# Padding the parts of a graph aggregation so that all its matmul operands begin at multiples of 64 bytes

## Chip, cores, metric

One core of one Trainium2 chip. The metric is the device time of one execution in microseconds (us). The kernel before takes 974.26 us (median of the 3 runs that were known when the prediction was made, 972.87 to 974.94); over all 6 runs of that comparison 973.04 us.

## The reference, cut to what matters

Two layers of attention over a graph of 4096 nodes with 512 features. Layer 0 attends inside 32 blocks of 128 nodes. Layer 1 is a graph attention with 8 heads of 64, in which the softmax over the neighbours j of node i needs only exp(t_j), because the term of i cancels:

```python
    def _L1_gnn_ref(x, adj, W, a_origin, a_dst):
        mx = jnp.einsum('nf,hfd->hnd', x, W)
        s_i = jnp.einsum('hnd,hd->hn', mx, a_origin)
        t_j = jnp.einsum('hnd,hd->hn', mx, a_dst)
        logits = s_i[:, :, None] + t_j[:, None, :]
        masked = jnp.where(adj[None] > 0, logits, neg_inf)
        attn = jax.nn.softmax(masked, axis=-1)
        out_h = jnp.einsum('hij,hjd->hid', attn, mx)
```

So layer 1 is a product of the 0/1 adjacency mask (4096 x 4096) with a matrix of 522 columns per node: 512 weighted features, 8 weights for the denominators and 2 of padding.

## The kernel before

A "part" is one tile of 128 nodes of that matrix, as a sum of two terms (high and low) of the 4-byte matmul type fp32r, in 3 chunks of 2 x 174 columns. The preparation makes the parts tile by tile: norm of the row (VectorE), transpose and projection with the weights (TensorE), weighing with exp(t) (VectorE), split into the two terms (ScalarE and GpSimd). The aggregation multiplies the transposed mask of a row of nodes (`at`, stationary) with all 32 parts (moving), 96 matmuls per row and 32 rows.

```python
CB = 3
CW1 = 174
EW = CB * CW1
# ... cut ...
    def split(e, dst):
        e3 = e.rearrange("p (c w) -> p c w", c=CB)
        nc.scalar.copy(dst[:, :, 0, :], e3)
        nc.gpsimd.tensor_sub(dst[:, :, 1, :], e3, dst[:, :, 0, :].bitcast(F32))
# ... cut: in aggregate, four loads of mw ...
        nc.vector.transpose(at8 ..., mw ...)          # arguments cut
        at = sb.tile([P, NT, P], F32R, name="at")
        nc.vector.tensor_copy(at ..., at8 ...)        # arguments cut
        pg = ps_g.tile([P, CB, 512], F32, name="pg")
        for j in range(NT):
            for c in range(CB):
                nc.tensor.matmul(
                    pg[:, c, : 2 * CW1], at[:, j, :],
                    part(j)[:, c].rearrange("p s w -> p (s w)"),
                    start=(j == 0), stop=(j == NT - 1),
                )
# ... cut ...
    with ExitStack() as straight:
        pool1 = straight.enter_context(tc.tile_pool(name="l1", bufs=1))
        sb2 = straight.enter_context(tc.tile_pool(name="sb2", bufs=2))
        lo = straight.enter_context(tc.tile_pool(name="lo", bufs=LO // 2))
        # ... cut: layer 0, and the preparation of the parts ...
        sb3 = straight.enter_context(
            tc.tile_pool(name="sb3", bufs=2, side="right", reuse_waits="tile")
        )
        for i in range(NT):
            row = sb3.tile([P, D], F32, name="row3", bufs=1)
            nc.sync.dma_start(row, x1_d[i])
            tot = aggregate(sb3, ps_g, i, lambda j: parts[j])
            # ... cut ...
            if i == 1:
                graphs_are_tiles(sb3)
                hold(0, rs_all, 1.0 / S_MAX, ALU.is_ge)
                # ... cut: three more range checks
```

A scheduler decides the order of the instructions on each engine, and the pools decide which buffers share addresses. Both matter below. If a check fails, a slow exact branch runs after the straight one.

Of the kernel before, what the change touches and what calls it, by code (L numbers as in the profile page):

```python
# [9 lines left out]
F32 = mybir.dt.float32  # L10
F32R = mybir.dt.float32r
# [9 lines left out]
P = 128  # L21
# [15 lines left out]
CB = 3  # L37
CW1 = 174
EW = CB * CW1
NEG = -1.0e6  # L40
EPS = 1e-5
SCALE = float(D) ** -0.5
# [9 lines left out]
def kernel(  # L52
# [185 lines left out]
    def project1(ps_m, hT, w1x):  # L238

        pm = [ps_m.tile([P, D], F32, name="pp") for _ in range(2)]  # L240
        for g, n in ((1, HW + H), (0, HW)):
            for k in range(KC):
                nc.tensor.matmul(  # L243
                    pm[g][:, :n], hT[:, k, :], w1x[:, k, g * HW : g * HW + n],
                    start=(k == 0), stop=(k == KC - 1),
                )
        return pm
# [11 lines left out]
    def aggregate(sb, ps_g, i, part):  # L259
# [21 lines left out]
        for j in range(NT):  # L281
            for c in range(CB):
# [4 lines left out]
                )  # L287
        tot = sb.tile([P, EW], F32, name="tot")
        tot3 = tot.rearrange("p (c w) -> p c w", c=CB)
# [8 lines left out]
    def graphs_are_tiles(sb):  # L298


        ptr_i = sb.tile([1, NPTR], I32, name="ptr_i", bufs=1)
        nc.sync.dma_start(ptr_i, ptr)
        ptr_f = sb.tile([1, NPTR], F32, name="ptr_f", bufs=1)
        nc.vector.tensor_copy(ptr_f, ptr_i)
        ends_i = sb.tile([1, NT, 2], I32, name="ends_i", bufs=1)
        nc.gpsimd.iota(ends_i, pattern=[[P, NT], [P - 1, 2]], base=0, channel_multiplier=0)
        ends = sb.tile([1, NT, 2], F32, name="ends", bufs=1)
        nc.vector.tensor_copy(ends, ends_i)
        ge = sb.tile([1, NT, 2], F32, name="ge", bufs=1)
        for t0 in range(0, NT, 4):  # L310
            cmp = sb.tile([1, 8, NPTR], F32, name="cmp", bufs=1)
            nc.vector.tensor_tensor(
                cmp,
                ends[:, t0 : t0 + 4].rearrange("p t e -> p (t e)")[:, :, None].to_broadcast(
                    [1, 8, NPTR]
                ),
                ptr_f[:, None, :].to_broadcast([1, 8, NPTR]),
                ALU.is_ge,
            )
            nc.vector.tensor_reduce(  # L320
                ge[:, t0 : t0 + 4].rearrange("p t e -> p (t e)"), cmp, AX.X, ALU.add
            )
        same = sb.tile([1, NT], F32, name="same", bufs=1)
        nc.vector.tensor_tensor(same, ge[:, :, 0], ge[:, :, 1], ALU.is_equal)
        later = sb.tile([1, NT - 1], F32, name="later", bufs=1)
        nc.vector.tensor_tensor(later, ge[:, 1:, 0], ge[:, : NT - 1, 1], ALU.is_gt)
        good = sb.tile([1, 2], F32, name="good", bufs=1)
        nc.vector.tensor_reduce(good[:, 0:1], same, AX.X, ALU.min)
        nc.vector.tensor_reduce(good[:, 1:2], later, AX.X, ALU.min)
        nc.vector.tensor_tensor(held[0:1, 6:7], good[:, 0:1], good[:, 1:2], ALU.mult)  # L330
# [8 lines left out]
    w1x = None  # L339
    parts = []  # L340
    with ExitStack() as straight:
        pool1 = straight.enter_context(tc.tile_pool(name="l1", bufs=1))
        sb2 = straight.enter_context(tc.tile_pool(name="sb2", bufs=2))
        lo = straight.enter_context(tc.tile_pool(name="lo", bufs=LO // 2))

        with ExitStack() as prep:
            ps_t = prep.enter_context(tc.tile_pool(name="ps_t0", bufs=3, space=PSUM))
            ps_p = prep.enter_context(tc.tile_pool(name="ps_p0", bufs=4, space=PSUM))

            def part_tile(pool, j):  # L350
                if j >= LO:
                    return pool.tile([P, CB, 2, CW1], F32R, name=f"part{j}")
                if j % 2 == 0:
                    two.append(pool.tile([P, 2, CB, 2, CW1], F32R, name=f"part{j}", tag="lo"))
                return two[-1][:, j % 2]

            two = []

# [8 lines left out]
            def prepare(i, hT, part):  # L367
                pm = project1(ps_p, hT, w1x)
                e = sb2.tile([P, EW], F32, name="e")
                nc.gpsimd.memset(e[:, EC:], 1.0)  # L370
# [6 lines left out]
            with (  # L377
# [49 lines left out]
                def read(i, diag, sums):  # L427
# [4 lines left out]
                    for h in range(2):  # L432
# [7 lines left out]
                        for c0, c1 in pieces:  # L440
                            if c0 < c1:
                                junk = sb.tile([P, NH], BF16, name="junk", bufs=1)
                                nc.scalar.activation(  # L443
                                    junk[:, c0:c1], a[:, c0:c1], AF.Exp, scale=2.0 * NEG,
                                    accum_out=sums[:, n : n + 1],
# [15 lines left out]
                def scores(g, hT, gT, r, diag, sums, counts):  # L461

                    pss = ps_s.tile([P, G, P], F32, name="pss")
                    for t in range(G):
                        for k in range(KC):
                            nc.tensor.matmul(  # L466
                                pss[:, t, :], gT[:, k, ts(t, P)], hT[:, k, ts(t, P)],
                                start=(k == 0), stop=(k == KC - 1),
                            )
                    s = sb.tile([P, G, P], F32, name="s")  # L470
                    nc.vector.scalar_tensor_tensor(s, diag, 2.0, pss, ALU.mult, ALU.add)
                    for t in range(G):
                        nc.scalar.activation(
                            s[:, t, :], s[:, t, :], AF.Exp, bias=r[:, t : t + 1],
                            accum_out=sums[t][:, 0:1],
                        )
                        rsum = rs_all[:, G * g + t : G * g + t + 1]
                        nc.vector.tensor_reduce(rsum, sums[t][:, : counts[t]], AX.X, ALU.add)
                        nc.vector.reciprocal(rsum, rsum)
                    return s  # L480
# [44 lines left out]
                for g in range(NG):  # L525
# [12 lines left out]
                    def prepare_on(now):  # L538
                        if now:
                            i = len(ahead)  # L540
                            ahead.append(normed1(i))
                            if i:
                                prepare(i - 1, ahead[i - 1], part_tile(lo, i - 1))

                    s = scores(g, hT, gT, r, *look)
# [23 lines left out]
            for i in range(n - 1, NT):  # L569
                hT = nhT  # L570
                if i + 1 < NT:
                    nhT = normed1(i + 1)
                prepare(i, hT, part_tile(lo if i < LO else hi, i))
# [16 lines left out]
        for i in range(NT):  # L590
# [21 lines left out]
# [3 lines that stand above are left out]
                hold(1, rs_all, 1.0 / S_MIN, ALU.is_le)  # L615
                e_flat = e_all.rearrange("p t h -> p (t h)")
                hold(2, e_flat, E_MIN, ALU.is_ge)
                hold(3, e_flat, E_MAX, ALU.is_le)
# [13 lines left out]
    with tc.If(bad > 0):  # L632
# [67 lines left out]
        with (  # L700
# [10 lines left out]
            with tc.For_i(0, NT, 1) as i:  # L711
# [8 lines left out]
                for c in range(N // CW):  # L720
# [12 lines left out]
                    f = sb.tile([P, CW], F32, name="f")  # L733
                    nc.vector.tensor_scalar(f, sm, 1.0 - NEG, NEG, ALU.mult, ALU.add)
                    nc.vector.tensor_tensor(ac, qk, f, ALU.mult)
# [7 lines left out]
                for c in range(N // CW):  # L743
# [7 lines left out]
                    for u in range(CW // P):  # L751
                        j = c * (CW // P) + u
# [11 lines left out]
        with (  # L764
# [60 lines left out]
            with tc.For_i(0, n_levels, 1):  # L825
                with (
# [11 lines left out]
                    nc.vector.tensor_scalar(te, te, 0.0, None, ALU.min)  # L838
                    e = sb.tile([P, EW], F32, name="e")
                    nc.gpsimd.memset(e[:, EC:], 1.0)  # L840
# [68 lines left out]
```

## Time and profile before

| what | before |
|---|---|
| time, median of 6 runs | 973.04 us |
| TensorE (PE) busy | 940.3 us of 970.5 us |
| aggregation, first to last matmul start | 468.74 to 958.04 us |
| one row of 96 matmuls | 15.293 us, 159.30 ns a matmul |
| last projection ends, to first aggregation matmul | 467.56 to 468.74 us |

The lines of the page that carry this stand in the prediction. Start times are those of the matmul records in the trace; the step from one start to the next is used because the end of a matmul is modelled. "Half clock" means a record of a granted TensorE clock of 0.5. "Seam" is the passage from the preparation to the aggregation.

One stretch of the timeline of before is needed for what follows (start, duration, engine, line, operation; in brackets the idle time before it and what ended it). It shows how work for the aggregation's second row sits in the middle of the preparation:

```profile
373.12 2.26 DVE L277 CAST at<-at 128x4096 fp32r<-128x4096 fp8e4 x1
...
376.06 0.65 DVE L114 BATCH_NORM_STATS2 stats<-row 128x6 f32<-128x512 f32 x1
...
377.64 1.44 DVE L121 TENSOR_SCALAR row<-row,mv,rstd 128x512 f32<-128x512 f32 x1 [0.94 <-POOL rstd L120]
...
379.14 1.12 PE L127 MATMUL pt<-ident,row 128*128 128x128 f32 x4 [3.02 <-DVE row L121]
```

The cast of `at` occupies VectorE (DVE) for 2.26 us, the norms of the next rows come after it, and PE waits 3.02 us for a normalised row. A half-clock record of 3.4 us follows from 378.7 us on.

### The profile page before, as it was taken

The numbers are of one execution on the slowest core, as the hardware profiler recorded it, in microseconds if no ns is written. First come the engines' busy times: TensorE is split into PE (matmuls) and PEld (weight loads), VectorE is DVE, ScalarE is ACT, GpSimd is POOL, SyncE is SP. The second block draws the span as 40 slices with busy tenths as digits, with TensorE's granted clock in tenths as the row PEclk, the third lists the DMA queues.
The fourth block names the chain that finished last, engine by engine and source line by source line (L and its number), as shares of the span: only waits on it lengthen the run. The fifth ranks groups of instructions, "written<-read, shape, count | busy, mean of one in ns | idle before, by whom it ended". The sixth has DMA issues, their size and how long they took to land.

```text
span 970.5 us, 13180 instructions
## 1 busy us (share of the span) xinstructions
PE 940.3 (97%) x5051; PEld 817.5 (84%) x5051; DVE 459.4 (47%) x978; ACT 260.7 (27%) x505; POOL 184.0 (19%) x344
## 2 busy tenths in 40 slices
PE   8999999989999998999999999999999999999995
PEld 5676677766677776788999999999999999999994
DVE  4678777866766358655133242433424233242321
ACT  5865666665762222233100000000000000000000
POOL 2211113231122125555110110101011010110100
PEclk9999999999999999999999999999999999999998
DMA  9989889898883033221022312223131221312201
GB/s 343 419 346 378 322 329 364 355 369 317 336 339 148 33 104 108 72 66 55 1 76 56 88 50 82 62 69 87 44 87 52 80 85 47 87 49 82 61 27 37
DMA packets 58042, 148.28 MB, mean 153 GB/s; under 512 B 6386, under 2 KB 23026, under 8 KB 49778
## 3 DMA queue, kind: packets, MB, share of 16 engines
q1 hardware_dynamic: 48178, 130.31, 38.3%
q10 hardware_dynamic: 9792, 17.05, 4.6%
q8 instruction: 41, 0.67, 0.3%
q14 instruction: 31, 0.25, 0.1%
HBM read 113.77 MB, written 33.55 MB: 152 GB/s over the span
## 4 chain that ended last, share of the span: by engine, by line
PE 89%; DVE 3%; DMA 2%; POOL 2%; ACT 2%; issue 1%; SPq 0%; ACTq 0%; DVEq 0%; POOLq 0%
PE pg L283 50%; PE pp L420 11%; PE pp L408 10%; PE pp L243 9%; PE pp L493 3%; PE pss L466 3%; PE pt L127 2%; DMA row<-x_d 1%; POOL part L231 1%; DMA xg<-x 1%; DVE a L136 1%; ACT junk L443 1%; DVE row L121 0%; DVE stats L114 0%; POOL rstd L120 0%
## 5 line engine op out<-in xcount | busy, mean ns | idle before, releaser
L283 PE MATMUL pg<-part,at 128*128 128x348 f32 x3072 | 489.6, 321 | 1.2 <-DVE e L252 1.2
L283 PEld LDWEIGHTS pg<-part,at 128*128 128x128 f32 x3072 | 489.4, 188 | 1.5 <-issue 1.5
L277 DVE CAST at<-at 128x4096 fp32r<-128x4096 fp8e4 x32 | 74.0, 2313 | 312.2 <-PE pg L283 312.2
L290 ACT COPY tot<-pg 128x522 f32<-128x522 f32 x32 | 19.2, 599 | 470.5 <-PE pg L283 470.5
L443 ACT ACTIVATE junk<-a 128x2048 bf16<-128x2048 f32 (+15 forms) x92 | 124.4, 1352 | 48.7 <-DVE x L495 28.0
L243 PE MATMUL pp<-w1x,hT 128*128 128x256 f32 (+1 forms) x512 | 118.4, 385 | 0.0
L420 PE MATMUL pp<-wv,hT 128*128 128x512 f32 x256 | 116.6, 600 | 0.0
L408 PE MATMUL pp<-hT,m_sb 128*128 128x256 f32 x512 | 113.2, 379 | 0.0
L243 PEld LDWEIGHTS pp<-w1x,hT 128*128 128x128 f32 x512 | 95.7, 192 | 13.6
L408 PEld LDWEIGHTS pp<-hT,m_sb 128*128 128x128 f32 x512 | 96.1, 190 | 12.9 <-issue 0.5
L420 PEld LDWEIGHTS pp<-wv,hT 128*128 128x128 f32 x256 | 49.1, 192 | 61.9 <-issue 61.9
L136 DVE TENSOR_SCALAR a<-a 128x512 fp8e4<-128x512 f32 x256 | 98.2, 460 | 0.5 <-DMA a_d<-a 0.4
L595 POOL COPY den_all<-tot 128x1 f32<-128x1 f32 x31 | 5.8, 186 | 369.1 <-DVE tot L291 369.1
L128 ACT ACTIVATE hT<-pt 128x512 f32<-128x512 f32 x64 | 37.0, 598 | 68.8 <-PE pt L127 68.7
L604 POOL TENSOR_TENSOR tot<-tot,row 128x512 f32<-128x512 f32 x31 | 40.0, 1290 | 61.7 <-DVE tot L296 61.7
L231 POOL TENSOR_TENSOR part<-e,part 128x522 fp32r<-128x522 f32 x32 | 42.1, 1316 | 43.0 <-ACT part L230 38.8
L118 POOL TENSOR_SCALAR ve<-mv 128x1 f32<-128x1 f32 x64 | 18.7, 295 | 150.9 <-DVE mv L116 150.8
L252 DVE TENSOR_TENSOR e<-pp,e 128x256 f32<-128x256 f32 x64 | 26.6, 417 | 28.9 <-ACT e L371 25.2
L270 DVE STREAM_TRANSPOSE at<-mw 128x1024 f32<-128x1024 f32 x32 | 39.5, 1236 | 0.0
L120 POOL TENSOR_TENSOR rstd<-ve,neghalf 128x1 f32<-128x1 f32 x64 | 38.5, 604 | 4.4
L424 DVE TENSOR_TENSOR v<-pp,bv_sb 128x512 f32<-128x512 f32 x32 | 22.0, 688 | 36.0 <-PE pp L420 36.0
L412 ACT ACTIVATE gT<-pp,c_sb 128x256 f32<-128x256 f32 x64 | 29.7, 468 | 29.4 <-PE pp L408 29.3
(93 smaller groups left out, 584.1 us busy)
## 6 DMA issues: line engine op xcount, KB each, us to landing
a<-adj SPq DMA_DIRECT2D x64, 1024.0 KB, 13.1
a_d<-a SPq DMA_DIRECT2D x32, 512.0 KB, 10.6
row<-x_d SPq DMA_DIRECT2D x64, 256.0 KB, 3.5
mw<-a_d SPq DMA_DIRECT2D x128, 128.0 KB, 4.0
xg<-x SPq DMA_DIRECT2D x16, 512.0 KB, 4.7
x_d<-x ACTq DMA_DIRECT2D x32, 256.0 KB, 4.2
out<-tot ACTq DMA_DIRECT2D x31, 256.0 KB, 3.8
wkT_sb<-wkT SPq DMA_DIRECT2D x4, 256.0 KB, 6.3
```

Of the source, the lines that this page charges most:

```text
L120: nc.gpsimd.tensor_tensor(rstd, ve, neghalf, ALU.pow)
L128: nc.scalar.activation(dst, pt, AF.Relu)
L136: nc.vector.tensor_scalar(a8v[:, u], av[:, u], 0.0, None, ALU.is_gt, saturate=False)
L231: nc.gpsimd.tensor_sub(dst[:, :, 1, :], e3, dst[:, :, 0, :].bitcast(F32))
L243: nc.tensor.matmul(pm[g][:, :n], hT[:, k, :], w1x[:, k, g * HW : g * HW + n], start=(k == 0), stop=(k == KC - 1),)
L270: nc.vector.transpose(at8.rearrange("p c n b -> p (c n b)").bitcast(F32).rearrange("p (c u n) -> p c u n", c=NW, n=B), mw.rearrange("p u ( ...
L277: nc.vector.tensor_copy(at.rearrange("p (c b) q -> p c b q", b=BY), at8.rearrange("p c q b -> p c b q"))
L283: nc.tensor.matmul(pg[:, c, : 2 * CW1], at[:, j, :], part(j)[:, c].rearrange("p s w -> p (s w)"), start=(j == 0), stop=(j == NT - 1),)
L408: nc.tensor.matmul(pp[:, : G * P], m_sb[:, k, ts(m, P)], hT[:, k, :], start=(k == 0), stop=(k == KC - 1),)
L420: nc.tensor.matmul(pp, hT[:, k, ts(t, P)], wv[:, k, :], start=(k == 0), stop=(k == KC - 1))
L443: nc.scalar.activation(junk[:, c0:c1], a[:, c0:c1], AF.Exp, scale=2.0 * NEG, accum_out=sums[:, n : n + 1],)
L604: nc.gpsimd.tensor_add(num, num, row)
```

## The change

The intent: let every moving operand (a chunk of a part) and every stationary operand (`at`) begin at a multiple of 64 bytes. A chunk of 348 floats gets the room of 352, and a two-element tile grows to 64 bytes so that what is allocated after it, `at` included, is aligned. The padded parts need 1.5 KB more per partition, for which the left-hand pools of layer 1's weights and norm buffers move to the right-hand side and end with the preparation.

```diff
+CP = 352
...
-        good = sb.tile([1, 2], F32, name="good", bufs=1)
+        good = sb.tile([1, 16], F32, name="good", bufs=1)
...
     with ExitStack() as straight:
-        pool1 = straight.enter_context(tc.tile_pool(name="l1", bufs=1))
-        sb2 = straight.enter_context(tc.tile_pool(name="sb2", bufs=2))
         lo = straight.enter_context(tc.tile_pool(name="lo", bufs=LO // 2))
 
         with ExitStack() as prep:
+            pool1 = prep.enter_context(tc.tile_pool(name="l1", bufs=1, side="right"))
+            sb2 = prep.enter_context(tc.tile_pool(name="sb2", bufs=2, side="right"))
...
             def part_tile(pool, j):
                 if j >= LO:
-                    return pool.tile([P, CB, 2, CW1], F32R, name=f"part{j}")
-                if j % 2 == 0:
-                    two.append(pool.tile([P, 2, CB, 2, CW1], F32R, name=f"part{j}", tag="lo"))
-                return two[-1][:, j % 2]
+                    t = pool.tile([P, CB, CP], F32R, name=f"part{j}")
+                else:
+                    if j % 2 == 0:
+                        two.append(pool.tile([P, 2, CB, CP], F32R, name=f"part{j}", tag="lo"))
+                    t = two[-1][:, j % 2]
+                return t[:, :, : 2 * CW1].rearrange("p c (s w) -> p c s w", s=2)
```

## The prediction

> **What bounds the kernel now.** I read the page's busy shares first, then its slices, its chain and its costliest groups, then waits and windows of single stretches.
>
> ```profile
> PE 940.3 (97%) x5051; PEld 817.5 (84%) x5051; DVE 459.4 (47%) x978; ACT 260.7 (27%) x505; POOL 184.0 (19%) x344
> ...
> PE   8999999989999998999999999999999999999995
> ...
> PE 89%; DVE 3%; DMA 2%; POOL 2%; ACT 2%; issue 1%; SPq 0%; ACTq 0%; DVEq 0%; POOLq 0%
> PE pg L283 50%; PE pp L420 11%; PE pp L408 10%; PE pp L243 9%; PE pp L493 3%; PE pss L466 3%; PE pt L127 2%; DMA row<-x_d 1%; POOL part L231 1%; DMA xg<-x 1%; DVE a L136 1%; ACT junk L443 1%; DVE row L121 0%; DVE stats L114 0%; POOL rstd L120 0%
> ...
> L283 PE MATMUL pg<-part,at 128*128 128x348 f32 x3072 | 489.6, 321 | 1.2 <-DVE e L252 1.2
> L283 PEld LDWEIGHTS pg<-part,at 128*128 128x128 f32 x3072 | 489.4, 188 | 1.5 <-issue 1.5
> L277 DVE CAST at<-at 128x4096 fp32r<-128x4096 fp8e4 x32 | 74.0, 2313 | 312.2 <-PE pg L283 312.2
> ```
>
> TensorE (PE) is busy for 97% of the span and is 89% of the chain that ended last. Half of the chain is one line, the aggregation's product: 3072 matmuls of 348 fp32r columns, which run from 468.7 us to 958 us with one wait of 1.2 us in front of them. Nothing feeds them late: the cast that makes their stationary operand waits 312 us in total for PE, not the other way round. So 489.6 us are set by the rate of that stream alone, and every nanosecond per matmul is worth 3.07 us.
>
> The windows view of L283, with the columns length, PE busy (count), PEld busy (count), granted clock, DMA share and GB/s, shows that the rate is steady:
>
> ```profile
> 500.00:600.00 100.00, 100.00 (x630) 100.00 (x629) 1.00 0.25 68
> 700.00:800.00 100.00, 100.00 (x629) 100.00 (x628) 1.00 0.25 72
> ```
>
> Some 628 starts in 100 us is 159.3 ns a matmul (first to last start: 489.3 us / 3071), at full granted clock. The starts in the trace repeat from row to row within a nanosecond: every row of 96 matmuls takes 15.293 us. That is not traffic from elsewhere; the matmuls' own operands decide it.
>
> Ahead of it, layer 1's preparation (projection L243, norm, split) also runs near PE's speed. Waits of PE from 345 to 500 us:
>
> ```profile
> PE pt L127 <- DVE row L121: 5.6, 4, 3.0
> PE pg L283 <- DVE e L252: 1.2, 1, 1.2
> ```
>
> **What the Trainium skill says.** (1) "TensorE: Matmul & The Clock Gate", section "Wait — 56ns, not 53.3ns?": back to back, a warm matmul costs N ÷ 2.4 GHz + about 2.5 ns. For N = 348 that is 147.5 ns. The trace has 159.3 ns, so 11.8 ns (36 us over the stage) are unexplained. The fp32 products of layer 0 have no such excess: 512 columns start 429 ns apart and 256 columns 216 ns apart, which is 2 clock cycles a column plus 2.3 ns. Only the fp32r stream, which takes a 4-byte column every cycle, falls behind. (2) "SBUF — State Buffer", section "Specifications (TRN2)": cachelines are 16 bytes. All operands of the products begin at multiples of 16 already, so this page gives the change no reason to help. (3) The same page, section "Operand start alignment", asks only for element alignment, and says of its runs that they timed nothing: no page states a gain at 64 bytes.
>
> **The change part by part.**
> *Alignment.* From the built programs: before, the 96 moving operands of a row begin at 0, 16, 32 and 48 bytes past a multiple of 64 (30, 18, 30 and 18 of them; a chunk is 348 x 4 = 1392 bytes = 21.75 x 64), and the stationary operand always at 32. After, all begin at 0. The count and the width of the matmuls stay. I sorted the time from each start to the next by where the moving operand begins: 159.0 ns at 0, 160.2 at 16, 159.5 at 32, 158.7 at 48. The third that is aligned already is not faster. Letting neighbours' alignments in too (a fit over the 96 matmuls of a row, each averaged over 29 rows) makes a fully aligned one 1.3 to 2.3 ns cheaper. Taken at face value that is 3/4 of about 1.5 ns x 3072 = some 3.5 us gained. What the trace can't tell is the stationary operand, since it is at 32 in all 3072 matmuls, nor what happens when both are aligned together.
> *The allocation.* The right-hand pools now hold layer 1's weights, norm and split buffers, and the aggregation's buffers lie over them. In the built order of before, the first two adjacency rows' transposes and casts, and the check of the graph's bounds, stand well inside the preparation. In that of after, all of them follow the last part. On DVE, after the last weighing: four pairs of the range checks (about 0.18 + 0.18 twice, 0.29 + 0.42 twice = 2.1 us), a copy that waits for an iota on GpSimd, which stands behind the last split (1.24 us, from 469.4 in the trace of before) and takes 0.27 us, then the transpose (1.23 us) and the cast (2.3 us). Chained onto before's times: last projection ends 467.6, last split ends about 470.3, iota 470.6, copy 470.8, the rest of the checks to 472.9, transpose to 474.1, cast (behind a small cast) to 476.8. The first aggregation matmul starts at 476.9 instead of 468.7: **+8.2 us**. The other copies are no trouble: 15.3 us of matmuls per row hide them.
> *What the move gives back.* Before, that early work on DVE delayed the norms: the two larger waits in the preparation are 3.0 us at 376.1 and 1.5 us at 395.2, and the first is followed by a record of half clock for 3.4 us, which costs 1.7 us of PE. Without the casts in the way up to 6.2 us come back; I count 4.5 of them.
> *The clock.* "TensorE: Matmul & The Clock Gate", section "What's actually happening", has idle windows of about 3.4 us bring the clock to half. The trace of before agrees: its idle spells of 2.5 and 3.0 us each precede 3413 ns at half clock. A spell of 9 us before the aggregation should do so too: + 1.7 us.
> Sum without a change of rate: 8.2 + 1.7 - 4.5 = +5.4 us; with the small gain of the fit, about +2 us.
> *The padded parts themselves* cost nothing in time: split's copies and subtractions write the same 522 elements, into three pieces as before.
>
> **The rivals.**
> A, the rate hardly moves (the sum above): 974 to 982 us. For it speaks that the aligned third isn't faster.
> B, the read of operands is the limit and counts 64-byte lines. A moving operand covers 22 or 23 of them (22.5 on average), a weight load at 32 covers 9, at 0 it covers 8. If 31.5 lines take 159.3 ns, 30 take 151.7 ns: 7.6 x 3.07 = 23 us gained, less 5: about 956 us. For it: only the stream with the doubled rate of bytes is short of its ideal, and the small, repeating differences between starts (152 to 168 ns) depend on addresses. Against it: parts that begin at 0 cover 68 lines in their three chunks and those at 32 cover 67, but the former are faster (476.7 against 479.1 ns).
> C, both operands aligned brings the ideal of 147.5 ns: 36 us gained, less 5, about 943 us. For it: the change goes to the length of widening a two-element tile to keep the stationary operand aligned too, which looks like knowledge of a measured effect. Against it: the trace shows nothing of it.
> D, the same phase in every pair of weight load and stream makes them collide more: 3 ns more would be 983 to 988 us. The address-dependent differences allow it.
> E, the aggregation starts late by more than I count, since a row's load or cast lands in the second row too: at most some 5 us more.
>
> **Range and chances.** I give A 0.6, B and C together (with what lies between) 0.33, D and E 0.07. A centres on 978 us, B and C on 945 to 957, some of it short of 2%. A gain of 2% needs under 954.8 us, thus about 25 us from the rate (8 ns a matmul): I take 0.28 for that. Slower by 2% needs over 993.7 us: 0.04. The middle of this lopsided mix is about 971 us; eight in ten between 942 and 985.
>
> **What would show it.** In the profile after: the L283 group's busy time (489.6 now; 485 to 490 under A, about 466 under B, about 453 under C) and the count of starts in 100 us (628; 659; 678). The wait of PE's first pg matmul should grow from 1.2 us to about 9 us, ended by the cast of at, with a half-clock record after it; the waits for DVE row L121 from 345 us on should shrink from 5.6 us to under 2. If the first pg wait stays under 3 us my reading of the moved order is wrong; if the repeating pattern of starts turns into one constant gap, the address-dependent part was alignment. The prediction fails mainly if the unexplained 11.8 ns do come from the stationary operand's place, which this trace cannot exclude.

## The result, and the profile after

| | before | after |
|---|---|---|
| time, median of 6 runs each | 973.04 us | 971.95 us |
| ratio of the fast runs, 95% interval | | 0.9987 (0.9974 to 1.0) |
| last projection ends | 467.56 us | 461.15 us |
| first aggregation matmul starts | 468.74 us | 469.81 us |
| first row of 96 | 15.37 us | 17.45 us |
| every later row of 96 | 15.293 us | 15.200 us |
| last aggregation matmul starts | 958.04 us | 958.30 us |

A ratio is the mean time of one kernel's fast runs over that of the other's in the same rounds, so it is not quite the ratio of the medians quoted. The time is the same within the noise. In later rounds, with 14 runs of the changed kernel against 19 of before, the ratio was 0.9995 (e12 below).

The page after, in the lines that answer to those in the prediction (TensorE's line number has moved from L283 to L284, the cast's from L277 to L278):

```profile
PE 938.7 (97%) x5051; PEld 816.8 (84%) x5051; DVE 459.2 (47%) x978; ACT 260.6 (27%) x505; POOL 177.0 (18%) x344
...
PE 92%; DVE 2%; DMA 2%; ACT 1%; issue 1%; POOL 0%; SPq 0%; DVEq 0%
...
L284 PE MATMUL pg<-part,at 128*128 128x348 f32 x3072 | 488.8, 321 | 8.7 <-DVE at L278 8.7
L284 PEld LDWEIGHTS pg<-part,at 128*128 128x128 f32 x3072 | 488.6, 188 | 9.0 <-issue 9.0
L278 DVE CAST at<-at 128x4096 fp32r<-128x4096 fp8e4 x32 | 73.4, 2292 | 298.2 <-PE pg L284 298.2
```

The aggregation's busy time is hardly shorter (488.8 against 489.6 us), but the idle time in front of it has grown from 1.2 to 8.7 us, and the cast of its first stationary operand ends it. PE's waits from 345 to 500 us were two lines before; after, they are one:

```profile
PE pg L284 <- DVE at L278: 8.7, 1, 8.7
```

The windows view of L284 shows the rate: 633 or 634 matmuls that overlap 100 us, where before it was 629 or 630.

```profile
500.00:600.00 100.00, 100.00 (x634) 100.00 (x633) 1.00 0.23 65
600.00:700.00 100.00, 100.00 (x633) 100.00 (x633) 1.00 0.26 73
```

The timeline of after where the preparation ends:

```profile
454.64 6.51 PE L244 MATMUL pp<-w1x,hT 128*128 128x264 f32 x29
...
462.43 1.22 POOL L232 TENSOR_TENSOR part<-e,part 128x522 fp32r<-128x522 f32 x1 [2.14 <-ACT part L231]
463.60 0.27 POOL L307 IOTA ends_i<- 1x64 int32 x1
463.91 0.18 DVE L309 CAST ends<-ends_i 1x64 f32<-1x64 int32 x1 [2.21 <-POOL ends_i L307]
...
466.10 1.24 DVE L271 STREAM_TRANSPOSE at<-mw 128x1024 f32<-128x1024 f32 x1
...
467.37 2.29 DVE L278 CAST at<-at 128x4096 fp32r<-128x4096 fp8e4 x1
...
469.81 8.43 PE L284 MATMUL pg<-part,at 128*128 128x348 f32 x38 [8.66 <-DVE at L278]
```

DVE stands idle for 2.21 us for the iota, which GpSimd (POOL) issues behind the last split; then come the range checks, the transpose and the cast, all while PE has nothing to do. The clock's records show half clock from 464.3 to 474.6 us, so the first 4.8 us of matmuls run slowly and the first row takes 17.45 us. The windows from 450 to 480 us, before and then after, show it in the granted clock (the third figure from the end):

```profile
450.00:480.00 30.00, 28.83 (x158) 26.22 (x157) 8.30 (x20) 5.49 (x13) 9.97 (x19) 1.00 0.05 18
```

```profile
450.00:480.00 30.00, 21.34 (x105) 19.57 (x104) 18.80 (x39) 4.01 (x9) 6.42 (x12) 0.83 0.16 42
```

**Where the time went**, from the two profiled runs: from the start of the fifth part's projection to the end of the last one, the preparation takes 140.8 instead of 148.9 us, -8.1 (its waits for the norms and their half clock are gone); the first matmul then waits 8.66 instead of 1.17 us, +7.5; the first row is 2.1 us longer; each of the other rows is 0.093 us shorter, -2.9 over 31 of them. The sum is -1.4 us, near the -1.1 us of the medians. In these two runs the last matmul starts 0.26 us later all the same, because the profiled run of after is already 1.7 us late when that fifth projection starts (320.4 against 318.7 us). This is not put down to the change: in the other profiled runs with the pools on the right that point lies anywhere from 316.0 to 320.6 us. Four effects of 2 to 8 us cancel.

### The profile page after: what moved, and what is told of

It is laid out like the page before. It is cut to its first block, busy times and chain, and to the rows that moved or that the text cites. A ratio compares the mean times of both kernels' runs of the same rounds, so it can differ in the third digit from the quotient of the medians.

```text
span 970.4 us, 13183 instructions
## 1 busy us (share of the span) xinstructions
PE 938.7 (97%) x5051; PEld 816.8 (84%) x5051; DVE 459.2 (47%) x978; ACT 260.6 (27%) x505; POOL 177.0 (18%) x344
## 4 chain that ended last, share of the span: by engine, by line
PE 92%; DVE 2%; DMA 2%; ACT 1%; issue 1%; POOL 0%; SPq 0%; DVEq 0%
PE pg L284 50%; PE pp L244 12%; PE pp L424 12%; PE pp L412 10%; PE pp L497 3%; PE pss L470 3%; PE pt L128 2%; DMA row<-x_d 1%; DMA xg<-x 1%; DVE a L137 1%; ACT junk L447 1%; ACT gT L416 0%; DVE wb L200 0%; DVE stats L115 0%; DMA bq_sb<-bq 0%
## 5 line engine op out<-in xcount | busy, mean ns | idle before, releaser
L284 PE MATMUL pg<-part,at 128*128 128x348 f32 x3072 | 488.8, 321 | 8.7 <-DVE at L278 8.7
L284 PEld LDWEIGHTS pg<-part,at 128*128 128x128 f32 x3072 | 488.6, 188 | 9.0 <-issue 9.0
L278 DVE CAST at<-at 128x4096 fp32r<-128x4096 fp8e4 x32 | 73.4, 2292 | 298.2 <-PE pg L284 298.2
L244 PEld LDWEIGHTS pp<-w1x,hT 128*128 128x128 f32 x512 | 94.9, 190 | 13.3
L119 POOL TENSOR_SCALAR ve<-mv 128x1 f32<-128x1 f32 x64 | 16.3, 258 | 163.5 <-DVE mv L117 163.5
```

Source lines behind the costliest of these rows:

```text
L244: nc.tensor.matmul(pm[g][:, :n], hT[:, k, :], w1x[:, k, g * HW : g * HW + n], start=(k == 0), stop=(k == KC - 1),)
L278: nc.vector.tensor_copy(at.rearrange("p (c b) q -> p c b q", b=BY), at8.rearrange("p c q b -> p c b q"))
L284: nc.tensor.matmul(pg[:, c, : 2 * CW1], at[:, j, :], part(j)[:, c].rearrange("p s w -> p (s w)"), start=(j == 0), stop=(j == NT - 1),)
```

## The experiments

All results were correct unless said otherwise. The timed ones (5 rounds: e1, e2, e3, e7, e11, e12) are in the fast state; by the mark of 2% only e11 differs from before, and the smaller differences are read from their intervals. The others are single runs, of which only rates and rows are read. What is said below of where operands begin was checked in the built programs. The theory at the start: alignment gains about 3 us in the rate, the move of the pools takes about as much back by reordering. The rival: the two belong together, or the alignment does nothing by itself.

### e1 and e2: the two halves of the change, each alone

e1 pads everything but keeps the pools on the left. To find the room, the aggregation's residual row borrows a norm buffer. Against the changed kernel:

```diff
+        pool1 = straight.enter_context(tc.tile_pool(name="l1", bufs=1))
+        sb2 = straight.enter_context(tc.tile_pool(name="sb2", bufs=2))
...
-            pool1 = prep.enter_context(tc.tile_pool(name="l1", bufs=1, side="right"))
-            sb2 = prep.enter_context(tc.tile_pool(name="sb2", bufs=2, side="right"))
...
-            row = sb3.tile([P, D], F32, name="row3", bufs=1)
+            row = sb2.tile([P, D], F32, name="row1")
```

> The alignment alone: parts and stationary operand padded as in the change, but layer 1's weight and norm buffers stay in the left-hand pools as in the kernel before (the aggregation's residual row borrows a norm buffer to make room). Theory (two opposite effects: rate gains 0.97 ns a matmul = 3 us, the move of the pools costs about 2 to 3 us): row of 96 matmuls 15.200 us as in the changed kernel, early casts and PE's waits for the norms back (5.6 us from 345 us on), wait of the first pg matmul about 1.2 us; 3 us faster than before, about 970 us. Rival (alignment does nothing by itself, the faster row comes from the new places of the buffers): row 15.29 us, time as before, 973 us.

e2 moves the pools but pads nothing:

```diff
-CP = 352
+CP = 2 * CW1
...
-        good = sb.tile([1, 16], F32, name="good", bufs=1)
+        good = sb.tile([1, 2], F32, name="good", bufs=1)
```

> The move of the pools alone: parts unpadded, stationary operand at 32 past a multiple of 64 as before. Theory: row 15.29 us as before, wait of the first pg matmul 8.7 us ended by the cast, about 10 us at half clock after it, no waits of PE for the norms from 345 us on; 1 to 4 us slower than before, 974 to 977 us. Rival (the move costs nothing): 973 us, and the gain of the changed kernel is the alignment's 1 us only.

e1 took 970.46 us against 972.46, ratio 0.9981 (0.9969 to 0.9994), with rows of 15.200 us. e2 took 974.25 us, ratio 1.0021 (1.001 to 1.0032), with rows of 15.293 us. PE's waits from 345 to 500 us, first in e1, then in e2:

```profile
PE pt L128 <- DVE row L122: 5.7, 4, 3.2
PE pg L284 <- DVE e L253: 1.2, 1, 1.2
```

```profile
PE pg L284 <- DVE at L278: 8.7, 1, 8.7
```

Each half behaves alone as it does in the whole: the waits go with the pools, the rate with the padding. The two ratios, -0.19% and +0.21%, cancel. Counted as above, e2's profile has -8.1 us in the preparation (140.8 us again), +7.5 for the wait and +2.3 for the first row: +1.7 us, against +1.8 of the medians. e1 gained 1.9 us rather than the expected 3. In its profiled run the aggregation was 2.97 us shorter, but the preparation ended at 470.0 instead of 467.6 us, with a half-clock record of 6.8 instead of 3.4 us. One run doesn't show whether that is usual for it.

### e3, e4, e8, e9: which operand's start matters

e3 lets the stationary operand fall back to 32 bytes past a multiple of 64 (`good` has two elements again); e4 lets every moving operand begin at 16. e8 rotates the stationary operand's start by row, and e9 does the same with all moving operands at 32.

```diff
# e4
-                return t[:, :, : 2 * CW1].rearrange("p c (s w) -> p c s w", s=2)
+                return t[:, :, 4 : 4 + 2 * CW1].rearrange("p c (s w) -> p c s w", s=2)
# e8 (and e9, with CP = 368 and the slice 8 : 8 + 2 * CW1)
-        at = sb.tile([P, NT, P], F32R, name="at")
+        at_wide = sb.tile([P, NT * P + 16], F32R, name="at")
+        off = 4 * (i % 4) if isinstance(i, int) else 0
+        at = at_wide[:, off : off + NT * P].rearrange("p (n q) -> p n q", q=P)
```

> The changed kernel with only the stationary operand back at 32 past a multiple of 64; all moving operands stay at 0. Theory (it is the uniform start of the moving operands that takes the irregular part of the gaps away): row within 0.02 us of 15.200. Rival (the stationary operand's place is what mattered): row 15.25 us or more. Time within 3 us of the changed kernel either way.

> The changed kernel with every moving operand at 16 past a multiple of 64 and the stationary at 0. If being at a multiple of 64 is what counts, the row of 96 is longer than 15.200 us, at least the 15.29 of before. If only the sameness of all starts counts, it stays within 0.02 us of 15.200.

> The changed kernel; the stationary operand begins at 0, 16, 32 and 48 past a multiple of 64 in rows 0, 1, 2, 3 and so on, all moving operands at 0. Theory relative (the gap depends on moving start less stationary start, modulo 64): rows 0 mod 4 take 15.20 us, 2 mod 4 15.36 us (both measured before), 3 mod 4 15.25 us (a difference of 16, as in the run with the moving operands at 16), 1 mod 4 about 15.38 us (worked out from the mixture of before: 159.30 = 0.3125 x 160.0 + 0.3125 x 158.33 + 0.1875 x 158.89 + 0.1875 x 160.2). Theory absolute (any start off 64 costs): all but rows 0 mod 4 take 15.25 us or more, in no set order.

> As the run before, but all moving operands at 32 past a multiple of 64. Theory relative: the fast rows are now those whose stationary operand is at 32 (rows 2 mod 4, 15.20 us), rows 0 mod 4 take 15.36 us, rows 1 mod 4 (difference 16) 15.25 us, rows 3 mod 4 about 15.38 us. Theory absolute (multiples of 64 are what counts): no row as fast as 15.20 us, and rows 2 mod 4 the slowest or equal to the others.

Measured, in ns from one start to the next (a row's duration over 96; the first row, in half clock, left out). A pair such as (32, 0) below is the moving start, then the stationary one:

| moving begins at | stationary at 0 | at 16 | at 32 | at 48 |
|---|---|---|---|---|
| 0 | 158.33 | 159.92 | 160.00 | 158.33 |
| 16 | 158.89 | | | |
| 32 | 159.74 | 159.72 | 159.96 | 159.95 |
| mixed, as before | | | 159.30 | |

The theory of e3 was wrong. With the moving operands aligned and the stationary one not, a row takes 15.360 us, which is more than the 15.293 of before. e3 took 976.39 us, ratio 1.0041 (1.0026 to 1.0056), some 4.5 us over the changed kernel (971.95 and 971.88 us in other rounds), where 3 at most were expected. The group line of e3 against 488.8 us of the changed kernel:

```profile
L284 PE MATMUL pg<-part,at 128*128 128x348 f32 x3072 | 494.0, 323 | 8.7 <-DVE at L278 8.7
```

So the 64 bytes given to a two-element tile are what makes the padding of the parts pay: without them the padding costs. e8 and e9 then refute both theories in their simple form. A rule of the difference between the two starts would have given 158.33 at (32, 32) and about 158.9 at (0, 48); they are 159.96 and 158.33. A rule that only multiples of 64 are fast fails at (0, 48) too. What stands is the table: aligned both ways is as fast as any pair tried, and the whole range is 1.7 ns, 1% of the stage. Two things besides the start modulo 64 differ inside the table. e9 has a different spacing of the parts. And in e8 and e9 the columns 16 and 48 come from the second of the two `at` buffers, which there begins at a multiple of 128, while the first one, and both buffers of the changed kernel, begin at 64 past one. So the table may carry more than the effect of the start modulo 64, and full alignment was tried at one place modulo 128 only. e4, e8 and e9 are single runs; their rows are read, not their times (974.04, 971.11 and 976.92 us against 969.16, 970.78 and 970.78 of before).

### e5, e6, e10: what the rest of the excess is

158.33 ns are 380 cycles at the 2.4 GHz that the prediction reckons with, for 348 columns streamed: an excess of 32 over one column a cycle. e5 and e6 were wrong on purpose: e5 loads 64 stationary columns instead of 128 in most steps, e6 streams 256 moving columns instead of 348.

```diff
# e5
-                    pg[:, c, : 2 * CW1], at[:, j, :],
+                    pg[: 64 if 0 < j < NT - 1 else P, c, : 2 * CW1],
+                    at[:, j, : 64 if 0 < j < NT - 1 else P],
# e6
-                    pg[:, c, : 2 * CW1], at[:, j, :],
-                    part(j)[:, c].rearrange("p s w -> p (s w)"),
+                    pg[:, c, : 2 * CW1 if j == 0 else 256], at[:, j, :],
+                    part(j)[:, c].rearrange("p s w -> p (s w)")[:, : 2 * CW1 if j == 0 else 256],
```

> Wrong result on purpose: in 30 of 32 steps the stationary operand has 64 columns instead of 128. Theory load (the 32 cycles by which 380 exceed 348 are proportional to the weights that a matmul loads): 364 cycles, 151.7 ns from start to start. Theory fixed or theory stream (a fixed turn-round of 32 cycles, or a stream that runs 9 per cent slow): 158.3 ns.

> Wrong result on purpose: in 31 of 32 steps the moving operand has 256 columns instead of 348. Theory load and theory fixed: 256 + 32 = 288 cycles, 120.0 ns from start to start. Theory stream (9.2 per cent slow): 279.5 cycles, 116.5 ns. Without any excess: 106.7 to 109 ns.

e5 measured 157.78 ns (mean of 48 consecutive matmuls of a row, over 23 rows), against 151.7 or 158.3: the excess isn't proportional to the weights loaded. The records of its weight loads did shrink, from 188 to 134 ns, while the step fell by 0.6 ns. Its checks failed, as its wrong numbers make them, and the slow branch ran (7365.66 us, relative error 0.23), so nothing but this rate is used. e6 (a single run, 850.8 us) has no one figure: its rows alternate. Over 72 consecutive matmuls, the rows that use the first `at` buffer take 116.67 ns a matmul, 280.0 cycles, close to the 279.5 of a proportional excess; the rows that use the second take 118.85 ns, 285.2 cycles, which is neither that nor the 288 of a fixed one. Both buffers begin at 0 modulo 64 and lie 16 KB apart, and the rows also write different PSUM banks; what makes the difference is open, and the changed kernel doesn't have it (158.33 ns in both kinds of row). So a fixed excess fits no row of e6, and a proportional one fits half of them. (e6 passed the comparison all the same: the columns that it leaves out hold low-order terms only.)

e10 takes half the bytes: the same matmuls with bf16 operands, a part being the sum of two bf16 terms.

```diff
-        at = sb.tile([P, NT, P], F32R, name="at")
+        at = sb.tile([P, NT, P], BF16, name="at")
...
-        nc.gpsimd.tensor_sub(dst[:, :, 1, :], e3, dst[:, :, 0, :].bitcast(F32))
+        nc.gpsimd.tensor_sub(dst[:, :, 1, :], e3, dst[:, :, 0, :])
# ... and F32R -> BF16 in the three tiles of parts
```

> The changed kernel with the aggregation's operands as bf16, stationary and moving (a part as a bf16 sum of two terms; less exact). The same count of matmuls and columns, half the bytes. Theory (the excess of about 11 ns over one column a cycle comes from reading 4-byte operands): 147 to 149 ns from start to start, row 14.1 to 14.3 us, some 33 us less in the aggregation. Rival (it is a cost of every weight load or turn-round, whatever the bytes): 158.3 ns, row 15.20 us.

The groups of e10, on TensorE:

```profile
L284 PE MATMUL pg<-part,at 128*128 128x348 bf16 x3072 | 456.0, 312 | 8.5 <-DVE at L278 8.5
L284 PEld LDWEIGHTS <-at 128*128 128x128 bf16 x3072 | 301.5, 98 | 163.0 <-DVE at L278 8.9
```

147.50 ns a matmul, row 14.160 us, 938.97 us in a single run against 970.78. Of the excess of 13.3 ns over 348 cycles, 2.5 are left. So the rest belongs to the 4-byte operands and not to the count or width of matmuls. Which of the two operands it comes from stays open: bf16 also halves the record of a weight load, from 188 to 98 ns. That e5's shorter weight loads changed almost nothing speaks for the moving operand, but no run has only one operand as bf16.

### e7, e11, e12: keeping the gain

e7 keeps the pools left as in e1, and queues on DVE the second row's transpose and cast, and the checks, behind the last weighing of the preparation. The first row's work stays early, where PE waits little for it.

```diff
-            nc.vector.tensor_tensor(
+            last_weigh[0] = nc.vector.tensor_tensor(
...
+        weighed = last_weigh[0].ins
...
-            tot = aggregate(sb3, ps_g, i, lambda j: parts[j])
+            with tc.issue_after(weighed) if i == 1 else ExitStack():
+                tot = aggregate(sb3, ps_g, i, lambda j: parts[j])
...
             if i == 1:
-                graphs_are_tiles(sb3)
+                with tc.issue_after(weighed):
+                    graphs_are_tiles(sb3)
# ... and the four range checks inside the same block
```

> The alignment with the pools left, and the DVE work of the second adjacency row and of the checks queued behind the last weighing, so that only the first row's transpose and cast run early. Theory (what is left to gain at the seam is PE's waits for the norms, and the half clock after the largest of them): no half clock near 380 us, wait of the first pg matmul 1 to 2 us, row 15.200 us; 7 to 10 us faster than before, 963 to 966 us. Rival (the waits for the norms came from something else than the second row's cast and the checks): waits of 4 us or more from 345 us on remain, time about 970 us.

e7 took 963.39 us, ratio 0.991 (0.9882 to 0.9939). Its waits of PE from 345 to 500 us:

```profile
PE pt L128 <- DVE row L122: 0.9, 1, 0.9
PE pg L286 <- DVE e L255: 0.6, 1, 0.6
```

There is no half clock between 222 and 952 us, the last projection ends at 461.36 us and the first aggregation matmul starts at 461.97. This keeps the earlier end of the preparation that the changed kernel has, and loses the late start that it paid with. The waits for the norms did come from the second row's work and the checks, which were moved together. Against e1, which has the same alignment and the same pools (970.46 us, same rounds), e7 is 7.1 us faster.

> The changed kernel once more, unaltered, in the same rounds as the next one. Theory (gains and losses nearly cancel): within 0.3 per cent of before, between 970 and 974 us. Rival (the first comparison's 0.13 per cent was chance and the late start costs more): 0.2 per cent slower or more.

e12, the changed kernel again: 971.88 us against 972.01, ratio 0.9995 (0.9985 to 1.0006). The first row again took 17.50 us and the first matmul again waited 8.7 us, so the late start is a property of the kernel.

e11 is e7 with the bf16 operands of e10; no other edit.

> Padding with the pools left, the second row's work and the checks queued behind the last weighing, and the aggregation's operands as bf16. Theory (the two gains are in different places and add up): row 14.16 us as in the run with bf16, wait of the first pg matmul about 1 us, no half clock near 380 us: 9 us from the seam and 33 us from the rate less than the changed kernel, 928 to 932 us. Rival (a faster stream runs into the casts or the rows' loads): rows longer than 14.2 us, 935 us or more.

e11 took 928.55 us, ratio 0.9556 (0.9537 to 0.9576), with rows of 14.160 us. It is correct by the comparison, but its operands have half the bytes and no error is on record for either kernel, so it is another kernel in that respect. The line of its group, against 488.8 us and 8.7 us of the changed kernel:

```profile
L286 PE MATMUL pg<-part,at 128*128 128x348 bf16 x3072 | 453.3, 311 | 0.5 <-DVE e L255 0.5
```

The gains of the seam and of the rate add up.

## Why the prediction was right, and where it was not

- **The bound** was read rightly: the change of the rate showed one to one in the stage (e1: 2.97 us of a row gain of 0.093 us x 32).
- **The size of the gain in rate** was right (0.97 ns a matmul, predicted about 1.1), but by luck, because the step that led to it was wrong. The fit over alignments of the moving operands said that an aligned one is 1.3 to 2.3 ns cheaper. e3 has all of them aligned with the stationary operand as in before, and is 0.7 ns *dearer*. What gave the gain is aligning the stationary operand with them, which the prediction named as the thing that the trace can't tell. The fit could not carry a size: redone on the trace of before, it makes an aligned operand 2.3 ns cheaper with one neighbour on each side, 1.0 with the one before only, and 3.0 ns dearer with the two after. (The share of operands that were not aligned is 66 of 96, so 0.69 and not 3/4.)
- **The late start** was read from the built order, and it came: a wait of 8.66 us where about 9 were expected, ended by the cast of `at`. The added idle time is 7.5 us, not 8.2: GpSimd's last split and iota came about 0.3 us sooner after the last projection than chained, and the small cast ahead of the large one took 0.13 us, about 0.4 us less than allowed for.
- **What the move gives back** was sized too small, and is the largest error of the sum: 4.5 of a possible 6.2 us were counted, and the preparation became 8.1 us shorter (140.8 us from the fifth projection on in after, e2, e3 and e12 alike), with no wait of PE left in it. The prediction left out the two smaller waits (0.4 and 0.6 us); the waits and the half clock add up to some 7 us, and the rest is not traced.
- **The clock** after the idle spell was sized too small: 1.7 us predicted from half-clock records of 3.4 us; the record lasted 10.2 us, 4.8 of them under matmuls, and the first row lost 2.25 us against the later ones. Nor does the trace of before agree with the page that the prediction cites, as it says it does: the idle spells of 2.5 and 3.0 us ahead of the half-clock records are shorter than the cited 3.4 us.
- **The sum** for this course was +2 us; the same terms in the profiles give -1.4, and the timed ratios are -0.13% and -0.05%. Course A's centre of 978 us lies between its two sums (+2 and +5.4 us), and its range of 974 to 982 us misses the 971.95 us by 2. That the stated middle of 971 us is so near is luck: it is the weighted middle of A with B and C, and these did not happen.
- **Rivals B and C** fall: counting 64-byte lines would give 151.7 ns, the ideal 147.5, and the aligned stream is at 158.33. e10 shows that 147.5 is reached with 2-byte operands. **D** falls with the result itself: the equal pair (0, 0) is 0.97 ns faster than the mixture of before, not 3 ns slower. But (32, 32) is 0.7 ns slower than that mixture, so equal starts alone decide nothing. **E** did not show: the second row took 15.200 us.
- **The repeating pattern** did not become one constant gap. It became a shorter one, of 155 to 161 ns.

## What to carry to other kernels

When a change needs room, look at what its new allocation does to the order of instructions: here a move of buffers cost 9.6 us and gave back 8.1, where the alignment itself gave 2.9, and putting the few early instructions where nobody waits for them was worth 7 us (e7 against e1). Where operand starts matter, measure pairs of stationary and moving starts: aligning the moving operands alone made it slower (e3); the stationary one alone, with the parts unpadded, was not tried. Before tuning 1% of a stream's rate, ask what its ideal is and what kind of operand keeps it from that; halving the bytes gave 7% of the stage.

## What the Trainium skill lacked or had wrong

- "TensorE: Matmul & The Clock Gate" gives N ÷ 2.4 GHz + about 2.5 ns without a word on fp32r. It holds for bf16 here (147.50 ns at N = 348), but fp32r matmuls of the same shape start 158.3 to 160.0 ns apart.
- "SBUF — State Buffer", section "Operand start alignment", times nothing. At these fp32r matmuls the start of the two operands modulo 64 bytes moves the rate between 158.33 and 160.00 ns, and the stationary operand's start counts as well.
- The first page's advice on idle time (section "Why this matters for your kernels") is about gaps over some 3 us. Here a wait of 2.5 us already comes just ahead of a half-clock record (at 214 us before, at 216 us after), and an idle spell of 8.7 us brought 10.2 us of half clock, of which 4.8 us fell on matmuls.
